# Four heads of ReLU attention weights on two engines: ScalarE takes a single bank and the pair, VectorE a bank of its own

## The chip, the cores and the metric

The kernel runs on one core of a Trainium2 chip. The metric is the device time of one execution in microseconds (us). A core has TensorE (PE, matrix products into PSUM), VectorE (DVE), ScalarE (ACT) and GpSimd (POOL), each with its own queue of instructions, and SyncE (SP), which issues DMAs. PSUM banks hold 128 x 512 numbers of four bytes here.

## The reference

Four layers follow each other on x of shape (4, 1024, 256): a gated attention in groups of 64, a low-rank feed-forward, a ReLU attention with 16 heads, and a mixture of eight experts. Each is wrapped as `x + layernorm(f(layernorm(x)))`. The change lies in the third:

```
scores = einsum('bhqd,bhkd->bhqk', q, k) / sqrt(16)
w = relu(scores)
attn = w / (sum(w, axis=-1) + 1e-6)
out = einsum('bhqk,bhkd->bhqd', attn, v)
y = layernorm(x + out @ w_out + b_out)
```

There are 4 rows (batch entries) of 1024 tokens, and 16 heads of width 16.

## The kernel before

**Stages.** The first two layers run to about 420 us of the span, the ReLU attention from there to about 1000 us, and the experts to the end. The attention is one long loop whose order is written out by hand for TensorE, VectorE and ScalarE: instructions stand in each engine's queue in the order in which the program calls them.

**Tiling.** For each of 4 rows there are 2 blocks of 512 queries, for each block 4 groups of 4 heads, and for each group 8 tiles of 128 keys: 256 steps in all. In the last block the queries are taken in two halves of 256, each with two key tiles in a step. `scores` (L1501) makes the scores of one step: 128 keys by 512 queries for each of four heads, in four PSUM banks. Two of them are single tiles of one bank (`singles`, tag `s`, a ring of three that the side work's small products share). The other two are one tile of two banks (`pair`, tag `d`, a ring of two). Then ReLU copies the scores into `w` in SBUF, a ring of three. `weigh` (L1527) multiplies `w` with the values into `po`, a single PSUM bank that collects the eight key tiles of a group. The values have a column of ones beside them, so `po` also holds the sums for the division.

**Order.** A step calls `scores` for itself and `finish` for the step two before. When the step that is finished is the last of its group, `finish` also transposes `po` into `turned` on VectorE (L1577). The first `weigh` of the next group overwrites `po` and must wait for that. Later parts of the same work divide by the sums (L1257 to L1259: `den`, `even`), transpose back (L1267: `oT`), project (L1288: `pt`), add and normalize (L1298 to L1320: `y`, `x`, with statistics at L1125 to L1132), and make the inputs of the experts' gate (L1349: `tpg`, L1352: `hTg`, L1364: `pg`). The next row's keys, queries and values (L392 to L441) are made in between. These parts wait in two lists: `beside` for pieces with TensorE work, `rest` for the others. A running account of how late each engine is (`late`, with costs written by hand) says when a part of `rest` may go.

**Heads by engine.** `heads_on_act` chooses how many of the four ReLUs ScalarE takes in a step:

```
if piece is not None and piece.tensor > 1.5:
    return 4
if late[1] > 0.0 or any(part.ready() and part.takes[1] for part in rest):
    return 2
return 3 if piece is None and at_end or last and len(rest) > 0 else 2
```

With a large side piece for TensorE it takes all four. It takes three where no piece is due and a group's last step is being finished, and in the last row while `rest` holds parts. Otherwise it takes two. The account's costs (`HEADS`) depend on that number. They are the same before and after.

With two heads, ScalarE takes the two singles (L1510) and VectorE the pair in one instruction (L1515). With four, ScalarE takes the singles and then the pair in one instruction (L1512). With three, ScalarE takes the singles and the first bank of the pair in three instructions (L1510), VectorE the second bank (L1515).

Of the kernel before, what the change touches and what calls it, by code (L numbers as in the profile page):

```python
# [13 lines left out]
AF = mybir.ActivationFunctionType  # L14
ALU = mybir.AluOpType
# [59 lines left out]
def kernel(  # L75
# [32 lines left out]
    nc = tc.nc  # L108
# [993 lines left out]
    with ExitStack() as st3:  # L1102
# [386 lines left out]
        def scores(row, qh, q2, halves, g, kt, on_act):  # L1489

            t, r = divmod(g, 2)
            n = TB // halves
            q0 = q2 * n
            w = wts.tile([P, 4, TB], F32, tag="w", name="w")
            singles = [ps.tile([P, TB], F32, tag="s", name="sc1", bufs=3) for _ in range(2)]
            pair = ps.tile([P, 2, TB], F32, tag="d", name="sc2", bufs=2)
            for m in range(halves):
                for part in (1, 0):
                    for j, sc in enumerate((*singles, pair[:, 0, :], pair[:, 1, :])):
                        rows = slice(32 * j, 32 * (j + 1))  # L1500
                        nc.tensor.matmul(  # L1501
                            sc[:, m * n : (m + 1) * n],
                            lhsT=row["kT"][t][rows, r, (kt + m) * P : (kt + m + 1) * P],
                            rhs=row["q"][qh, t][rows, r, part, q0 : q0 + n],
                            start=(part == 1),
                            stop=(part == 0),
                        )

            for j, sc in enumerate((*singles, pair[:, 0, :])[: 2 if on_act == 4 else on_act]):
                nc.scalar.activation(w[:, j, :], sc, AF.Relu)  # L1510
            if on_act == 4:
                nc.scalar.activation(w[:, 2:4, :], pair, AF.Relu)  # L1512
            else:
                j = on_act - 2
                nc.vector.tensor_scalar(w[:, 2 + j : 4, :], pair[:, j:2, :], 0.0, None, ALU.max)  # L1515
            return w

        def weighed(halves, r):
# [94 lines left out]
        def ends(at):  # L1613

            return at[6] == KT - at[4]

        def heads_on_act(piece, at_end, last):
# [6 lines that stand above are left out]
# [8 lines left out]
        for b in range(B):  # L1632
            after = open_row(None if b else next_hs, last=b + 2 == B) if b + 1 < B else None
            for qh in range(BPB):
# [13 lines left out]
                for q2 in range(halves):  # L1648
                    for g in range(NG):
                        for kt in range(0, KT, halves):  # L1650
                            Part.now += 1
                            piece = piece_for(waiting[0]) if len(waiting) > 1 else None
                            on_act = heads_on_act(piece, len(waiting) > 1 and ends(waiting[0]), row["last"])
                            w = scores(row, qh, q2, halves, g, kt, on_act)
                            waiting.append((row, b, qh, q2, halves, g, kt, w))
                            step = kt // halves
                            if step == 1 and g % 2 == 0:
                                if g == 0 and q2 == 0:
                                    fetch_queries(row, qh, 1)
                                elif g and halves == 1:  # L1660
                                    fetch_queries(*((row, 1) if qh == 0 else (after, 0)), 0)
                            for i, us in enumerate(HEADS[on_act]):
                                late[i] -= us
                            if len(waiting) > 2:
                                go_on_with_oldest(piece)
                            else:
                                go_on()
                            late[:] = [max(x, 0.0) for x in late]
# [574 lines left out]
```

## Time and profile before

| | before |
|---|---|
| median of 3 runs (lowest to highest) | 1534.33 us (1531.61 to 1535.67) |
| profiled execution: its time / its span | 1538.66 / 1536.9 us |
| mean granted TensorE clock | 0.984 |
| busy share of the span: PE, DVE, ACT, POOL | 95%, 57%, 46%, 32% |
| attention, 420 to 1000 us: PE, DVE, ACT busy | 551.1, 408.0, 400.9 of 580 us |
| steps with two, three, four heads on ScalarE | 152, 53, 51 |

A row of the profile names the source line, the engine, the operation, the tiles as out<-in, the shape and the count; then the busy time in us and the mean in ns, then how long the engine was idle just before these instructions, and what ended most of that. The page has the busy parts, the queues, the chain that ended last and the costliest groups. The trace also answers for a stretch: busy time, who waited for whom, and the instructions in order of time. A time of day such as 479.54 is counted in us from the start of the span. "PE po L1527 <- DVE turned L1577" reads: the matmuls into `po` at line 1527 waited for VectorE's write of `turned` at line 1577.

### The profile page before, as it was taken

The page shows a single profiled execution, that of the slowest core. Times are in us where ns is not written, and L with a number is a line of the kernel's source. Part 1 is how long each engine was busy: PE and PEld are TensorE (multiplying, and loading weights), DVE is VectorE, ACT ScalarE, POOL GpSimd, SP SyncE. Part 2 cuts the span into 40 slices and gives each one's busy share as a digit, 9 for nine tenths or more (in the row PEclk, how much of TensorE's full clock was granted, in tenths as well). Part 3 has the DMA queues.
Part 4 walks back from the last instruction along what each step waited for, and adds up shares of the span by engine and source line. Part 5 has one row for each costly group of instructions (what it writes and reads, how often), then busy time and mean ns, then how long its engine had stood idle before and what let it go on. Part 6 is the DMA issues. An engine that isn't in the chain of part 4 may idle for free. (4 is left out here: it accounts for less than half of the span.)

```text
span 1536.9 us, 24162 instructions
## 1 busy us (share of the span) xinstructions
PE 1465.8 (95%) x9286; PEld 787.5 (51%) x9286; DVE 875.4 (57%) x2140; ACT 701.4 (46%) x1201; POOL 495.9 (32%) x627
## 2 busy tenths in 40 slices
PE   8999999999899999999999999859999999999996
PEld 4666666666432323332333224427656765665674
DVE  5455664556456588648874776775545631222145
ACT  4244455443466666766676787622121112112142
POOL 4122233223341214311432223303425243242554
PEclk9999999999999999999999999969999999999999
DMA  8400000003323221532154210151314233233264
GB/s 217 128 1 1 1 1 0 1 0 126 121 71 124 90 91 61 173 114 87 49 165 138 70 56 29 40 158 36 99 22 122 49 70 90 56 79 78 63 161 127
DMA packets 91886, 121.59 MB, mean 79 GB/s; under 512 B 24925, under 2 KB 64250, under 8 KB 91642
## 3 DMA queue, kind: packets, MB, share of 16 engines
q1 hardware_dynamic: 70000, 73.09, 15.1%
q0 software_dynamic: 21712, 46.94, 13.0%
q8 instruction: 73, 1.20, 0.3%
q14 instruction: 43, 0.35, 0.1%
q10 hardware_dynamic: 58, 0.01, 0.0%
HBM read 66.90 MB, written 53.12 MB: 78 GB/s over the span
## 5 line engine op out<-in xcount | busy, mean ns | idle before, releaser
L1510 ACT ACTIVATE w<-sc 128x512 f32<-128x512 f32 x565 | 303.8, 596 | 135.1 <-issue 44.4
L1527 PE MATMUL po<-w,vaug 128*17 128x512 f32 (+1 forms) x2304 | 271.6, 553 | 24.3 <-DVE turned L1577 24.2
L1515 DVE TENSOR_SCALAR w<-sc 128x1024 f32<-128x1024 f32 (+1 forms) x205 | 221.2, 1083 | 77.1 <-ACT w L1510 43.7
L2125 ACT ACTIVATE hid<-ph,mb 128x512 f32<-128x512 f32 (+1 forms) x136 | 90.0, 662 | 340.0 <-PE ph L2118 249.6
L2118 PE MATMUL ph<-xT,w 128*128 128x512 f32 (+1 forms) x544 | 229.6, 574 | 0.3 <-DVE xT L2101 0.3
L2135 PE MATMUL py<-w,hid 128*128 128x256 f32 x1024 | 229.7, 380 | 0.0
L2135 PEld LDWEIGHTS py<-w,hid 128*128 128x128 f32 x1024 | 191.8, 190 | 31.6 <-issue 7.0
L1501 PE MATMUL sc<-q,kT 32*128 32x512 f32 (+1 forms) x2304 | 192.2, 414 | 2.7 <-ACT vaug L441 1.0
L1501 PEld LDWEIGHTS sc<-q,kT 32*128 32x128 f32 x2304 | 86.8, 184 | 176.4 <-ACT w L1510 112.6
L2156 POOL DMA_INDIRECT acc_d<-y,idx x56 | 88.8, 1585 | 225.5 <-DVE y L2155 111.1
L2118 PEld LDWEIGHTS ph<-xT,w 128*128 128x128 f32 x544 | 99.8, 190 | 107.1 <-issue 98.1
L1527 PEld LDWEIGHTS po<-w,vaug 128*17 128x17 f32 x2304 | 41.8, 95 | 118.8 <-issue 72.3
L2154 DVE TENSOR_TENSOR y<-py,mb 128x256 f32<-128x256 f32 x56 | 23.5, 420 | 125.9 <-PE py L2135 116.5
L1926 POOL DMA_INDIRECT got<-tok_d,idx x64 | 66.3, 1037 | 62.6 <-DVE counts L1760 24.4
L724 PE MATMUL pg<-nT,wh 128*128 128x512 f32 x128 | 61.1, 610 | 1.5 <-ACT nT L663 1.5
L2101 DVE COPY xT<-tp 128x512 f32<-128x512 f32 (+1 forms) x34 | 22.2, 659 | 70.7 <-PE tp L2096 64.6
L850 PE MATMUL py<-wo,oT 128*128 128x256 f32 x256 | 61.9, 385 | 0.0
L740 PE MATMUL pv<-wh,nT 128*128 128x512 f32 x128 | 59.7, 593 | 0.0
L850 PEld LDWEIGHTS py<-wo,oT 128*128 128x128 f32 x256 | 47.3, 190 | 17.1 <-issue 9.6
L1512 ACT ACTIVATE w<-sc 128x1024 f32<-128x1024 f32 x51 | 52.7, 1032 | 0.0
L915 ACT ACTIVATE hid<-ph,vec 128x512 f32<-128x512 f32 x64 | 39.8, 685 | 27.4 <-PE ph L906 27.2
L588 POOL TENSOR_TENSOR x<-x,y 128x1024 f32<-128x1024 f32 x13 | 30.6, 2353 | 57.4 <-ACT y L577 57.3
(307 smaller groups left out, 2043.5 us busy)
## 6 DMA issues: line engine op xcount, KB each, us to landing
q<-q_d POOLq DMA_DIRECT2D x16, 1024.0 KB, 6.4
w<-in_L_ffn_W_dram SPq DMA_DIRECT2D x16, 1024.0 KB
q_d<-parts SPq DMA_DIRECT2D x48, 256.0 KB
kT<-k_d POOLq DMA_DIRECT2D x16, 512.0 KB, 4.1
k_d<-parts SPq DMA_DIRECT2D x24, 256.0 KB
acc_d<-logits SPq DMA_DIRECT2D x8, 512.0 KB
tok_d<-hg SPq DMA_DIRECT2D x32, 128.0 KB
x<-in_L_attn_x_dram SPq DMA_DIRECT2D x7, 512.0 KB
```

Of the source, the lines that this page charges most:

```text
L724: nc.tensor.matmul(pg, lhsT=wh[:, c, HID + e * P : HID + (e + 1) * P], rhs=d["nT"][:, c, :], start=(c == 0), stop=(c == DC - 1),)
L740: nc.tensor.matmul(pv, lhsT=d["nT"][:, c, i * P : (i + 1) * P], rhs=wh[:, c, 0:HID], start=(c == 0), stop=(c == DC - 1),)
L850: nc.tensor.matmul(py, lhsT=d["oT"][:, e, :], rhs=wo[:, e, :], start=(e == 0), stop=(e == EC - 1))
L1501: nc.tensor.matmul(sc[:, m * n : (m + 1) * n], lhsT=row["kT"][t][rows, r, (kt + m) * P : (kt + m + 1) * P], rhs=row["q"][qh, t][rows, r, p ...
L1510: nc.scalar.activation(w[:, j, :], sc, AF.Relu)
L1515: nc.vector.tensor_scalar(w[:, 2 + j : 4, :], pair[:, j:2, :], 0.0, None, ALU.max)
L1527: nc.tensor.matmul(po[32 * j : 32 * j + HD + 1, weighed(halves, r)], lhsT=row["v"][:, kt + m, HQ * t + 4 * r + j, :], rhs=w[:, j, m * n : ...
L1926: return nc.gpsimd.indirect_dma_start(out=dst, out_offset=None, in_=rows[:, :], in_offset=self.at_chunk(c), bounds_check=NT - 1, oob_is_er ...
L2118: nc.tensor.matmul(ph, lhsT=w1[:, c, f * P : (f + 1) * P], rhs=xT[u][:, c, h * n : (h + 1) * n], start=(c == 0), stop=(c == DC - 1),)
L2125: nc.scalar.activation(hid[:, f, h * n : (h + 1) * n], ph, AF.Gelu, bias=mb1[:, e * FC + f : e * FC + f + 1])
L2135: nc.tensor.matmul(py, lhsT=hid[:, f, i * P : (i + 1) * P], rhs=w2[:, f, :], start=(f == 0), stop=(f == FC - 1),)
L2156: scatter = nc.gpsimd.indirect_dma_start(out=acc_d[:, :], out_offset=lists[e].at_chunk(k), in_=y, in_offset=None, bounds_check=NT - 1, oob ...
```

## The change

In a step with three heads on ScalarE, ScalarE takes the first single bank and then the whole pair in one instruction of 128 x 1024, and VectorE takes the second single bank. Before, ScalarE took both singles and the first bank of the pair in three instructions, and VectorE the pair's second bank. Steps with two and four heads keep their instructions. The choice of the number of heads, and with it the order of all other work, is as before.

```
-            for j, sc in enumerate((*singles, pair[:, 0, :])[: 2 if on_act == 4 else on_act]):
-                nc.scalar.activation(w[:, j, :], sc, AF.Relu)
-            if on_act == 4:
+            nc.scalar.activation(w[:, 0, :], singles[0], AF.Relu)
+            if on_act == 3:
+                nc.vector.tensor_scalar(w[:, 1, :], singles[1], 0.0, None, ALU.max)
+            else:
+                nc.scalar.activation(w[:, 1, :], singles[1], AF.Relu)
+            if on_act > 2:
                 nc.scalar.activation(w[:, 2:4, :], pair, AF.Relu)
             else:
-                j = on_act - 2
-                nc.vector.tensor_scalar(w[:, 2 + j : 4, :], pair[:, j:2, :], 0.0, None, ALU.max)
+                nc.vector.tensor_scalar(w[:, 2:4, :], pair, 0.0, None, ALU.max)
             return w
```

## The prediction

> **What bounds the kernel now.** I read the page's first part, then busy time by stretch, then who waited for whom, and last the timeline around one such wait. TensorE is busy nearly all the span:
>
> ```profile
> PE 1465.8 (95%) x9286; PEld 787.5 (51%) x9286; DVE 875.4 (57%) x2140; ACT 701.4 (46%) x1201; POOL 495.9 (32%) x627
> ```
>
> So only TensorE's idle time can be won unless its work changes, and the edit changes none of that. The edited lines run from 420 to 1000 us. Four stretches of that stage add up to:
>
> ```profile
> sum 580.00, PE 551.13 PEld 198.53 DVE 407.97 ACT 400.92 POOL 172.67; mean PE 137.78 PEld 49.63 DVE 101.99 ACT 100.23 POOL 43.17
> ```
>
> TensorE idles 580.0 - 551.1 = 28.9 us there: no gain can be much larger. Its waits, in the view of waits by engine over that stage, begin with one line that holds nearly all of it; below it are VectorE's, from the same view (us in total, times, longest):
>
> ```profile
> PE po L1527 <- DVE turned L1577: 24.2, 22, 1.5
> ...
> DVE w L1515 <- ACT w L1510: 43.7, 42, 2.0
> DVE w L1515 <- PE sc L1501: 31.8, 45, 3.0
> ```
>
> TensorE waits 22 times for `turned`, the transpose that empties `po` before the next group of heads may overwrite it. VectorE in its turn waits 42 times for ScalarE's ReLU. The groups by shape say which VectorE ReLU that is:
>
> ```profile
> L1510 ACT ACTIVATE w<-sc 128x512 f32<-128x512 f32 x565 | 303.8, 596 | 135.1 <-issue 44.4 <-ACT w L1510 41.7 <-PE sc L1501 37.3
> L1515 DVE TENSOR_SCALAR w<-sc 128x1024 f32<-128x1024 f32 x152 | 184.8, 1220 | 33.3 <-PE sc L1501 31.8 <-ACT hT L393 0.4
> L1512 ACT ACTIVATE w<-sc 128x1024 f32<-128x1024 f32 x51 | 52.7, 1032 | 0.0
> L1515 DVE TENSOR_SCALAR w<-sc 128x512 f32<-128x512 f32 x53 | 36.6, 690 | 43.8 <-ACT w L1510 43.7
> L1577 DVE STREAM_TRANSPOSE turned<-po 128x512 f32<-128x512 f32 x28 | 19.8, 708 | 5.5 <-PE po L1527 5.5
> ```
>
> The 53 one-bank ReLUs are the steps with three heads on ScalarE (152 have two, 51 four). They alone wait for ScalarE; the 152 two-bank ones wait for the matmuls. The timeline of one such step shows the chain:
>
> ```profile
> 477.12 0.74 PE L1501 MATMUL sc<-q,kT 32*128 32x512 f32 x8
> 477.78 1.05 PE L1527 MATMUL po<-w,vaug 128*17 128x512 f32 x8
> 477.93 1.58 ACT L1510 ACTIVATE w<-sc 128x512 f32<-128x512 f32 x3 [0.57 <-ACT w L1510]
> 478.76 0.74 PE L1501 MATMUL sc<-q,kT 32*128 32x512 f32 x8
> 479.54 0.69 DVE L1515 TENSOR_SCALAR w<-sc 128x512 f32<-128x512 f32 x1 [1.95 <-ACT w L1510]
> ...
> 480.15 0.71 DVE L1577 STREAM_TRANSPOSE turned<-po 128x512 f32<-128x512 f32 x1
> 480.91 1.05 PE L1527 MATMUL po<-w,vaug 128*17 128x512 f32 x8 [1.41 <-DVE turned L1577]
> ```
>
> The scores are complete at 477.86 and `po` at 478.83, but VectorE starts its ReLU at 479.54, when the third ScalarE ReLU has ended (479.51), and `turned` stands behind it. TensorE has finished the next scores at 479.50 and stands for 1.41 us.
>
> **What the Trainium skill says.** "PSUM — Partial Sum Buffer", section on bank collisions: two engines may not touch one bank and quadrant at a time, but on different banks they run clean together. The trace agrees: two-bank ReLUs run on VectorE beside ScalarE's at 1.22 and 0.60 us. Nothing in the banks thus demands the 1.6 us wait, which goes with the shared tile `pair`. The same page, "Engine vs sequencer instructions": the queues of ScalarE and VectorE are strict FIFO; so `turned` cannot pass the waiting ReLU, as seen above. "ScalarE: Activation LUTs", "What ACT_TABLE_LOAD costs": an ACTIVATE with immediates takes 186 ns + 0.833 ns per element, and neighbours overlap by about 93 ns. That gives 612 and 1039 ns; the trace has 596 and 1032.
>
> **The change part by part.** Only the 53 three-head steps change. The built order of instructions is otherwise the same on every engine: TensorE, POOL and SP keep all their instructions and DMAs, and nothing moves past anything.
>
> (1) *ScalarE*: 3 x 0.596 becomes 0.596 + 1.032; less overlaps of about 0.11 (three in 1.58 us above) 1.58 becomes 1.52, so 53 x 0.06 = 3 us of ScalarE time. Worth 0: it idles 0.57 us ahead of such a step.
>
> (2) *VectorE's ReLU* keeps its size (0.69 us), but reads a tile of its own. In the built program it waits for its matmul and for the older user of its `w` buffer, no longer for this step's ScalarE. It can start some 0.15 us after the matmuls (a two-bank one started at 476.36 after scores that ended at 476.20): 478.0 in place of 479.54. It ends at 478.7, before `po` is complete. Then `turned` starts 0.07 after `po` (elsewhere 461.79 to 461.86), takes 0.71, and TensorE follows 0.05 later: 478.83 + 0.83 = 479.66. TensorE is due at 479.50, so 0.16 of the 1.41 stays: **what is late next is `turned` itself**.
>
> *Stretch 420 to 860.* Of 13.6 us in 12 stalls, 0.54 and 0.22 stand behind another VectorE queue (two-bank ReLUs) and stay. Ten follow a three-head ReLU, 12.9 us: eight of 1.40 or 1.41, two of 0.81, where TensorE has other work between and nothing stays. Ahead of all ten VectorE had waited for ScalarE at least 1.19 us. Saved: 12.9 - 8 x 0.16 = 11.6.
>
> *Stretch 860 to 1000* (the last row, 43 of the 53 steps; 10 stalls, 10.6 us). One stall of 0.74 follows two-bank ReLUs. Nine follow a three-head one: 1.48, 0.82, 1.35, 1.35, 1.07, 1.07, 1.08, 1.12, 0.47, 9.8 together. Here VectorE also has layer-norm work, and its wait ahead of the nine ReLUs was only 0, 0.54, 0.12, 0.38, then 1.57, 0.97, 0.76, 1.56, 0.17. Capped by these and by the end of `po`, 5.1 go. But earlier ReLUs of the stretch waited too (27.8 us in 32 waits), and that time moves the queue up: with it all go but 0.16 in three places and a little elsewhere, 9.3. I take 8, nearer the upper end, because the queue before the four weakest shows ReLUs that waited 1.83, 1.13, 0.82 and 0.60.
>
> (3) *Other waits behind the same ReLU*: 0.74 as named; 0.53 (`sc` for `y`, at 974.17), 0.25 (`pt` for `oT`, at 933.68); and the hand-over at 995.05, where the ReLU waited 0.70 and the last layer-norm chain runs behind it. From 0 to 2.2; I take 1.5.
>
> (4) *New waits.* In the built order 28 score matmuls and 7 of the side work's (`tpg`, `pt`, `tp`) now wait for VectorE's ReLU where they waited for ScalarE's, as the single bank is released there; 29 lose a wait for VectorE on `pair`. Scores reuse it two steps (3.3 us) later: hidden behind two steps of TensorE work. The side work may come about 1 us later. No row shows its cost: at least 0 (a gain beyond (2) has no source), at most 7 x 0.5 = 3.5 if VectorE is half a us late every time. I take 1.
>
> Sum: 11.6 + 8 + 1.5 - 1 = **20 us**. Against the profiled execution, 1538.7 us (span 1536.9 and 1.8 around it), that is 1518.7; it ran 4.3 above the median, 1534.3, which goes to **1514.3**. After 1000 us the work depends on TensorE's arrival, so the gain is carried to the end.
>
> **The rivals.** (A) *VectorE's own queue takes the wait's place* in the last row: only the stretch before 860 gains, less 1 to 3 for new waits: 9 to 11, about 1524. For it: 11 of the 53 ReLUs did not wait. Against: the 27.8 us of waits there. (B) *No measurable change*: VectorE still waits for ScalarE, through `w`, which both still write. Then only part (1) is left and the time is 1534. Against: in two-head steps both write one `w` and VectorE waits only for TensorE. (C) *Slower*: the single bank, now released by VectorE, is late where ScalarE's was not. It decides once VectorE reaches its ReLU over 1 us late for side work, or 2.5 us late for scores: 35 waits at 1 us cost 35 against the 20, about 1549. For it: VectorE is 70% busy in this stage. Against: today's `pair` is released by VectorE later still, and no stall of TensorE names it.
>
> **How the numbers follow.** Forecast 0.76, A 0.12, B 0.06, C 0.06. The forecast's ends: 11.6 + 5.1 + 0 - 1 = 15.7, and 11.6 + 9.3 + 2.2 = 23.1: 1511 to 1519. With A's centre and 2 us by which runs scatter (1531.6 to 1535.7) it becomes 1509 to 1523. A measurement of this kernel tells about 0.3%, 4.6 us, from no change: faster 0.88 (forecast and A), same 0.06, slower 0.06.
>
> **What would show it.** Right: the one-bank VectorE ReLU waits for `sc` and not for ScalarE; "po <- turned" falls from 24.2 to some 5 us, mostly pieces of 0.1 to 0.2, and 0.54 and 0.22 remain; TensorE's busy time stays near 1466. Wrong: "DVE w <- ACT w" still near 40 us (B); stalls after 860 as long as now with VectorE busy before them (A); new stalls of `tpg`, `pt` or `sc` for VectorE's `w` (C).

## The result, and the profile after

The changed kernel takes 1510.5 us (median of 4 runs, 1508.3 to 1511.9); beside it the kernel before took 1535.0 (4 runs, 1531.6 to 1538.3). The ratio is 0.9839, with a 95% interval from 0.9814 to 0.9865: 24.5 us faster, with the interval 21 to 29. The forecast was 20 us and 1514.3, in a range from 1509 to 1523: the time lies inside the range, and the gain is larger than forecast. The profiled execution took 1511.9 us (span 1510.1, before 1536.9).

The new code is two lines longer, which shifts the line numbers: line 1527 of before is 1529 now, the transpose is at 1579, and the ReLUs are at 1509 and 1513 (ScalarE, one bank), 1515 (ScalarE, pair), 1511 (VectorE, one bank) and 1517 (VectorE, pair). First the busy time of the page:

```profile
PE 1461.7 (97%) x9286; PEld 786.1 (52%) x9286; DVE 876.1 (58%) x2140; ACT 698.2 (46%) x1148; POOL 496.5 (33%) x627
```

TensorE has the same 9286 matmuls and nearly the same busy time in 26.8 us less span. ScalarE has 53 instructions and 3.2 us less, as part (1) of the prediction had it. The waits of the attention stage, TensorE's first, then VectorE's (us in total, times, longest):

```profile
PE po L1529 <- DVE turned L1579: 2.6, 13, 0.5
...
DVE turned L1579 <- PE po L1529: 9.7, 20, 1.4
...
DVE w L1511 <- PE sc L1501: 5.9, 15, 1.0
```

TensorE waited 24.2 us for the transpose and now waits 2.6 (the forecast was some 5). "DVE w <- ACT w", 43.7 us before, is gone from the view; the one-bank ReLU waits for its matmul. And the transpose now waits for `po` in 20 places, 9.7 us (before 5.9 us in 7): the order of who is late has turned round. The groups by shape:

```profile
L1515 ACT ACTIVATE w<-sc 128x1024 f32<-128x1024 f32 x104 | 106.7, 1026 | 0.0
L1511 DVE TENSOR_SCALAR w<-sc 128x512 f32<-128x512 f32 x53 | 36.5, 688 | 6.7 <-PE sc L1501 5.9 <-ACT hTg L1352 0.4
L1579 DVE STREAM_TRANSPOSE turned<-po 128x512 f32<-128x512 f32 x28 | 20.0, 713 | 7.8 <-PE po L1529 7.7
```

VectorE's ReLU is no faster (688 ns against 690), it has only lost its wait: 6.7 us idle ahead of the 53, where there were 43.8. The step that the prediction showed, in the timeline after (start, duration, then the instruction):

```profile
475.60 0.74 PE L1501 MATMUL sc<-q,kT 32*128 32x512 f32 x8
...
476.27 1.05 PE L1529 MATMUL po<-w,vaug 128*17 128x512 f32 x8
476.42 0.60 ACT L1509 ACTIVATE w<-sc 128x512 f32<-128x512 f32 x1 [0.57 <-ACT w L1513]
476.46 0.69 DVE L1511 TENSOR_SCALAR w<-sc 128x512 f32<-128x512 f32 x1 [0.39 <-PE sc L1501]
476.91 1.02 ACT L1515 ACTIVATE w<-sc 128x1024 f32<-128x1024 f32 x1
...
477.39 0.72 DVE L1579 STREAM_TRANSPOSE turned<-po 128x512 f32<-128x512 f32 x1 [0.24 <-PE po L1529]
...
478.16 1.05 PE L1529 MATMUL po<-w,vaug 128*17 128x512 f32 x8 [0.17 <-DVE turned L1579]
```

Both engines start within 0.04 us of each other. The ReLU is done at 477.15, `po` at 477.32, and the transpose starts 0.07 later. Of the stall of 1.41 us 0.17 is left (0.16 was forecast).

**Where the time came from.** TensorE's matmuls are the same in number and order, so the two traces can be laid side by side, matmul by matmul; how far the second is ahead gives the gain up to any point.

| up to | ahead by, us | gained in between | what |
|---|---|---|---|
| 430 us of before | 1.5 | 1.5 | the granted clock, 0.85 from 424 to 444 us in the profile before, 0.93 in the one after |
| 849.4 (836.3 after) | 13.1 | 11.6 | ten stalls behind three-head ReLUs |
| 998.2 (971.5 after) | 26.7 | 13.6 | the last row: 9.7 in nine stalls, 3.9 elsewhere |
| the end | 26.8 | 0.1 | the experts: carried through |

The first 1.5 us are no work of the change: no three-head step lies there (the first is at 479.5 us of before).

### The profile page after: what moved, and what is told of

Its sections match the earlier page's. It is cut to its first block, busy times and chain, and to the rows that moved or that the text cites. A ratio compares the mean times of both kernels' runs of the same rounds, so it can differ in the third digit from the quotient of the medians.

```text
span 1510.1 us, 24181 instructions
## 1 busy us (share of the span) xinstructions
PE 1461.7 (97%) x9286; PEld 786.1 (52%) x9286; DVE 876.1 (58%) x2140; ACT 698.2 (46%) x1148; POOL 496.5 (33%) x627
## 5 line engine op out<-in xcount | busy, mean ns | idle before, releaser
L1517 DVE TENSOR_SCALAR w<-sc 128x1024 f32<-128x1024 f32 x152 | 185.1, 1222 | 36.2 <-PE sc L1501 33.8
L1509 ACT ACTIVATE w<-sc 128x512 f32<-128x512 f32 x256 | 152.9, 597 | 113.7 <-ACT w L1513 49.5
L1513 ACT ACTIVATE w<-sc 128x512 f32<-128x512 f32 x203 | 120.2, 592 | 0.0
L1515 ACT ACTIVATE w<-sc 128x1024 f32<-128x1024 f32 x104 | 106.7, 1026 | 0.0
L1928 POOL DMA_INDIRECT got<-tok_d,idx x64 | 66.6, 1041 | 62.9 <-DVE counts L1762 24.5
```

What stands on the lines that cost most here:

```text
L1509: nc.scalar.activation(w[:, 0, :], singles[0], AF.Relu)
L1513: nc.scalar.activation(w[:, 1, :], singles[1], AF.Relu)
L1517: nc.vector.tensor_scalar(w[:, 2:4, :], pair, 0.0, None, ALU.max)
L1928: return nc.gpsimd.indirect_dma_start(out=dst, out_offset=None, in_=rows[:, :], in_offset=self.at_chunk(c), bounds_check=NT - 1, oob_is_er ...
```

## The experiments

Each is timed against the kernel before. The first four ran together, as did the next four and the last two. Only the code of the three-head step or its place is shown; the line numbers differ by a few from kernel to kernel.

### 1. The old sharing, VectorE called first

```
+            if on_act == 3:
+                nc.vector.tensor_scalar(w[:, 3, :], pair[:, 1, :], 0.0, None, ALU.max)
             for j, sc in enumerate((*singles, pair[:, 0, :])[: 2 if on_act == 4 else on_act]):
                 nc.scalar.activation(w[:, j, :], sc, AF.Relu)
             if on_act == 4:
                 nc.scalar.activation(w[:, 2:4, :], pair, AF.Relu)
-            else:
-                j = on_act - 2
-                nc.vector.tensor_scalar(w[:, 2 + j : 4, :], pair[:, j:2, :], 0.0, None, ALU.max)
+            elif on_act == 2:
+                nc.vector.tensor_scalar(w[:, 2:4, :], pair, 0.0, None, ALU.max)
```

> The heads are shared out as before (ScalarE both singles and the pair's first bank in three instructions, VectorE the pair's second bank), but in a three-head step VectorE's ReLU is called ahead of ScalarE's. Theory (what cost the time was VectorE's wait for ScalarE, with the transpose of po behind it in VectorE's queue): the wait goes though the pair is still shared, TensorE's wait for the transpose falls from 24 us to 2 to 4 us, and the time is 1510 to 1514. Rival (a shared pair holds one engine up in either order): now ScalarE's third ReLU waits for VectorE's wherever VectorE is late, in about a fifth of the 53 steps by half a us or more, scores behind it come later, and the time is 1516 to 1522.

1509.0 us, ratio 0.9828 (0.9808 to 0.9849). VectorE's one-bank ReLU in the groups by shape, and one of ScalarE's waits:

```profile
L1510 DVE TENSOR_SCALAR w<-sc 128x512 f32<-128x512 f32 x53 | 36.4, 688 | 7.7 <-PE sc L1501 6.5 <-ACT hTg L1352 0.4 <-ACT w L1512 0.3
...
ACT w L1512 <- DVE w L1510: 2.4, 6, 0.7
```

The pair is still shared, VectorE reads one bank of it while ScalarE works on other banks, and the whole gain is there; TensorE waits 2.6 us for the transpose, as in the changed kernel. So a bank of its own is one way, not the reason: what counts is that VectorE does not come after ScalarE. It was the order of the two calls on one tile that had made VectorE the later. The tile still ties the two engines, now the other way round: in all 53 steps ScalarE's third ReLU begins only after VectorE's has ended (0.03 us later at the least). So the rival of this run does appear, but small: ScalarE stands for VectorE 2.4 us in six waits, where half a us in a fifth of the steps was its claim, and scores come visibly late behind it in one place only (near 933 us, 0.45 us). VectorE's ReLU mostly ends before ScalarE has finished its first two.

### 2. The new sharing, the pair in two ScalarE instructions

```
-            if on_act > 2:
+            if on_act == 3:
+                for j in range(2):
+                    nc.scalar.activation(w[:, 2 + j, :], pair[:, j, :], AF.Relu)
+            elif on_act == 4:
                 nc.scalar.activation(w[:, 2:4, :], pair, AF.Relu)
```

> The changed kernel, with the pair in a three-head step taken by ScalarE in two instructions of one bank rather than one of two. Theory (ScalarE's shorter work is worth nothing, the whole gain is the wait): ScalarE is 3 us busier, the time is within 1.5 us of the changed kernel's 1510.5. Rival (part of the gain is ScalarE's shorter step, above all in the last row where three-head steps follow each other at 1.58 us against TensorE's 1.65): 2 to 3 us slower, 1513.

1509.3 us, ratio 0.9829 (0.9812 to 0.9846), against 0.9839 for the change. The shorter ScalarE step is worth nothing that can be measured; with experiment 1 this leaves VectorE's wait as the cause of the gain, as far as the times can tell.

### 3. The change in the first three rows only

The first branch holds the new sharing, the second the old.

```
+            if not row["last"]:
...
+            else:
...
```

> The change in the first three rows only (10 steps); the last row keeps the old sharing (43 steps). Theory: ten stalls of 12.9 us shrink to eight of 0.17; with 0.1 us more for each stall where the pipeline had run dry, the time falls by 12 to 13 us, to 1522 to 1523. Rival (more than half of the gain comes from the last row's lighter VectorE queue): a fall of 8 us or less, 1527 or more.

1524.2 us, ratio 0.9922 (0.9906 to 0.9939): 10.4 us less in the medians, 9.4 to 14.4 by the interval. In its trace the eight stalls are 0.17 each and those of the last row stay as they were (1.49, 0.82, 1.35, 1.35, 1.07 and so on). TensorE's wait and one of VectorE's:

```profile
PE po L1538 <- DVE turned L1588: 12.7, 20, 1.5
...
DVE w L1526 <- ACT w L1521: 27.8, 32, 1.9
```

27.8 us in 32 waits is what the last row had in the kernel before. Laid side by side, the traces of the kernels before and after gave 11.6 for these ten steps; the time is 1.2 us above the expected 1523. The extra 0.1 us a stall that I had expected was not there in the eight stalls that shrank to 0.17 (1.41 to 0.17 brought 1.24); the two that went altogether gave 0.07 each (0.81 brought 0.88). The rival's "8 or less" lies outside the interval. So nearly half of the gain comes from ten steps, the rest from the last row's 43.

### 4. The change only where the transpose follows

The branches as in experiment 3; `group_end` is true where the step that is finished is the last of its group.

```
+            if group_end:
...
+            else:
...
```

> The change only in the 19 three-head steps with the transpose behind VectorE's ReLU; the other 34 of the last row keep the old sharing. Theory (VectorE's freed time carries over in the last row from one step to the next): four stalls of the last row stay for the most part (about 0.9, 0.3, 1.2 and 1.0 us, as VectorE comes to them late), and so do those behind other work; 4 to 6 us slower than the changed kernel, 1515 to 1517. Rival (only the ReLU ahead of each transpose matters): within 1.5 us of the changed kernel, 1511.

1514.0 us, ratio 0.9867 (0.9846 to 0.9888), 4.7 to 5.0 behind experiments 1 and 2, which ran with it: the theory holds, and the time lies just under the expected 1515 to 1517. One of the last row's stalls, in the timeline:

```profile
847.09 0.48 DVE L1320 SCALAR_TENSOR_TENSOR x<-y,rsc,x 128x256 f32<-128x256 f32 x1
847.48 0.69 DVE L1512 TENSOR_SCALAR w<-sc 128x512 f32<-128x512 f32 x1
848.09 0.71 DVE L1588 STREAM_TRANSPOSE turned<-po 128x512 f32<-128x512 f32 x1
...
848.85 0.62 PE L1538 MATMUL po<-w,vaug 128*17 128x512 f32 x4 [1.49 <-DVE turned L1588]
```

Here the ReLU has the new sharing and waits for nobody, but VectorE comes to it late, and TensorE still stands 1.49 us. In the changed kernel the same stall is 0.17. The earlier ReLUs' waits had made VectorE late: freed time does carry over from step to step.

### 5. Two heads on ScalarE in place of three

```
-                            w = scores(row, qh, q2, halves, g, kt, on_act)
+                            w = scores(row, qh, q2, halves, g, kt, 2 if on_act == 3 else on_act)
```

> The kernel before, with ScalarE taking two heads in the 53 steps where it took three (VectorE the whole pair in one instruction of 1.22 us, which waits for no ScalarE); the account of lateness and all else stay. Theory (in a wait-free step only VectorE's load and the end of po count): in the first three rows the ReLU ends 0.53 us later than in the changed kernel, the transpose about 0.25 later, and eight stalls of 0.17 become 0.41: 10 us saved there. In the last row VectorE gets 43 x 0.53 = 23 us more, on a queue that was already late in four stalls of nine, so little or nothing is saved there: 1521 to 1530. Rival (three heads on ScalarE are not needed at all once nothing waits for ScalarE): within 3 us of the changed kernel, 1510 to 1513.

1522.3 us, ratio 0.9916 (0.9897 to 0.9935). The first three rows gain nearly as expected (six of the eight stalls are 0.41 to 0.56, two 0.65 and 0.67; matmul by matmul 8.8 us where 10 were expected). In the last row VectorE is full; the stretch from 860 to 990 us (its length, then busy us of PE, PEld, DVE, ACT, POOL, each with its count; last the granted clock, the share of DMA and GB/s):

```profile
860.00:990.00 130.00, 121.49 (x1572) 55.07 (x1565) 114.70 (x226) 77.69 (x142) 44.06 (x83) 0.99 0.14 45
```

VectorE is busy 114.7 of 130 us, and stalls of 1.81, 1.25 and 1.03 us stand there. The third head on ScalarE is needed, but only without the wait: even two heads beat the old three.

### 6. The old sharing, the transpose ahead of the ReLU

In three-head steps at a group's end VectorE's ReLU, wait and all, is called behind the transpose:

```
-                nc.vector.tensor_scalar(w[:, 2 + j : 4, :], pair[:, j:2, :], 0.0, None, ALU.max)
+                held.append(
+                    lambda: nc.vector.tensor_scalar(w[:, 2 + j : 4, :], pair[:, j:2, :], 0.0, None, ALU.max)
+                )
+                if not (on_act == 3 and group_end):
+                    held.pop()()
...
                     po[:, weighed(halves, r)],
                 )
+                while held:
+                    held.pop()()
```

> The kernel before with its sharing of heads, but in three-head steps at a group's end VectorE's ReLU is called behind the transpose of po, not ahead of it; it still waits for ScalarE. Theory (the wait cost time only because the transpose stood behind it in the queue): TensorE's waits for the transpose fall as in the changed kernel in the first three rows (0.17 each) and to about 0.1 to 0.9 in the last row, where VectorE is late; VectorE still waits 20 to 40 us for ScalarE; 1512 to 1517. Rival (the ReLU's own lateness holds the later weighing): 1525 or more.

1514.4 us, ratio 0.9872 (0.9852 to 0.9892). TensorE hardly waits, and part of VectorE's wait for ScalarE is left. Below the waits, the step that the prediction showed:

```profile
PE po L1533 <- DVE turned L1583: 4.6, 14, 0.9
...
DVE w L1518 <- ACT w L1512: 16.9, 26, 1.9
...
475.07 0.74 PE L1503 MATMUL sc<-q,kT 32*128 32x512 f32 x8
475.20 0.72 DVE L1583 STREAM_TRANSPOSE turned<-po 128x512 f32<-128x512 f32 x1 [1.31 <-PE po L1533]
475.84 0.69 DVE L1518 TENSOR_SCALAR w<-sc 128x512 f32<-128x512 f32 x1
...
475.97 0.62 PE L1533 MATMUL po<-w,vaug 128*17 128x512 f32 x4 [0.17 <-DVE turned L1583]
```

20 of the 24 us come back. VectorE's ReLU begins no earlier than it did, 0.77 us after TensorE's next scores (478.76 and 479.54 in the kernel before, 0.78), but the transpose now lies in the time that VectorE had stood waiting, and TensorE's 1.41 us become 0.17. At the 19 group ends VectorE thus stands idle for ScalarE only 0.4 us in all, 22.0 before. The 16.9 us that are left (20 to 40 were expected) stand nearly all at steps with no transpose behind the ReLU; they still make VectorE late in the last row, where stalls of 0.89, 0.54 and 0.31 us stay. The wait cost time by what stood behind it in VectorE's queue.

### 7. The change, with every ReLU behind the transpose

At each group's end, in two-head steps too, the ReLU is called behind the transpose, by the same `held` list in the changed kernel.

> The changed kernel, and VectorE's ReLU called behind the transpose of po at every group's end, in two-head steps too. Theory (0.17 us of each stall is the transpose itself after po's end): the stalls of 0.54 and 0.22 behind two-head ReLUs go, those of 0.17 stay; 1 us at most, so no difference that can be measured, 1508 to 1511. Rival (a later ReLU makes scores wait for its bank): 1513 or more, with waits of sc for VectorE's w.

1515.2 us, ratio 0.9868 (0.9848 to 0.9888): a miss, 4.7 us above the changed kernel's own median. The two did not run together and the intervals of their ratios overlap, so the reading rests on the traces. The stalls of 0.54 and 0.22 went as expected, but new ones came (timeline):

```profile
575.84 0.72 DVE L1583 STREAM_TRANSPOSE turned<-po 128x512 f32<-128x512 f32 x1 [0.57 <-PE po L1533]
...
576.48 0.65 DVE L1513 TENSOR_SCALAR w<-sc 128x512 f32<-128x512 f32 x1
...
577.28 0.63 PE L1349 MATMUL tpg<-ident,hg 128*128 128x128 f32 x4 [0.84 <-DVE w L1513]
```

The gate's transposes take the single bank that this ReLU empties, and the ReLU now comes late. This is the prediction's rival C at work, in the side work and not in the scores: 0.84 us for `tpg`, 0.84 for `tp`, and only one wait of 0.15 for scores. In the changed kernel, with the ReLU first, no idle time of TensorE's matmuls is put down to L1511. Of 3.9 us between the two profiled executions 1.6 were there before the first wait for the transpose, 1.3 of them from 424 to 431 us, where the granted clock dips, and are no work of the edit.

### 8. The change only where no transpose follows

The condition of experiment 4 turned round.

> The change only in the 34 three-head steps without a transpose behind VectorE's ReLU; the 19 at a group's end keep the old sharing. Theory (the loss sits in the ReLU ahead of the transpose): all stalls of 1.0 to 1.5 us stay at 1.1 to 1.5, only the waits of pt and sc for VectorE and some of the end go; 1530 to 1534. Rival (a lighter VectorE queue is itself worth half of the last row's 13 us): 1528 or less.

1532.3 us (14 runs), ratio 0.9987 (0.9975 to 0.9998).

```profile
PE po L1538 <- DVE turned L1588: 24.3, 21, 1.4
...
DVE w L1526 <- ACT w L1521: 31.3, 19, 2.5
```

The freed 34 steps alone bring about 2 us (0.3 to 3.8 by the interval). The stalls behind three-head ReLUs stay, at 1.1 to 1.4 each (0.8 in three). The 19 ReLUs that are still held waited 31.3 us for ScalarE, 1.65 each, where they had waited 22.0 in the kernel before: what is freed ahead of a held ReLU is spent waiting there. With the 19 freed as well, the same 34 are worth 3.5 to 5 us (experiment 4 against the change and against experiments 1 and 2).

### 9 and 10. Two-head steps reordered, beside the changed kernel again

In the changed kernel, only the nine two-head steps at a group's end have the ReLU behind the transpose.

> The changed kernel, with VectorE's ReLU called behind the transpose only in the nine two-head steps at a group's end (three-head steps keep it ahead). Theory (the stalls of 0.54 and 0.22 come from the two-bank ReLU ahead of the transpose, and the side work's new waits only from a one-bank ReLU called late): both stalls go, no wait of tpg or tp for VectorE's w appears, 0.8 to 1 us less in the trace, too little for the times to show: within 1.5 us of the changed kernel run beside it. Rival (any later ReLU holds the scores): 2 us or more slower.

> The changed kernel itself, on the same chip as the nine-step variant. Theory: 1508 to 1512, TensorE's waits for the transpose 2.6 us in all, as in its first profile; what differs between executions is the stretch just after 424 us, where the granted clock dips, by 1 to 4 us. Rival (the first profile was a lucky one): 1514 or more.

1512.9 us, ratio 0.9846 (0.9829 to 0.9863), beside the changed kernel's 1512.1, 0.9836 (0.9819 to 0.9853). No difference can be measured. The stalls of 0.54 and 0.22 went, but one of 0.17 became 0.36, a new one of 0.15 (`sc` for VectorE's `w`) came, and `tpg` waited 1.2 us for POOL near the end where it had waited 0.6; the trace ends 1.1 us later, not 0.8 to 1 earlier. The changed kernel's repeat shows the 2.6 us of its first profile; its time is 24.7 below that of the kernel before on that chip (1536.8). None of these versions is measurably better than the changed kernel.

## Why the prediction was right, point by point

**The mechanism** stood as told: ScalarE's third ReLU, VectorE's ReLU, the transpose, TensorE. Experiments 1 and 6 break that chain at two different places without the change and get all of the gain (25.6 us) and most of it (19.8). The sizes were less good: three terms missed, all on the same side.

**Part (1)**, ScalarE worth 0: shown by experiment 2.

**Part (2), 420 to 860 us:** 11.6 forecast, 11.6 in the aligned traces. The remainder of 0.16 measured 0.17, and it is the transpose, as said: it now waits for `po`.

**Part (2), the last row:** 8 forecast, 9.7 measured. This term was too small. The carry-over was complete: all nine stalls fell to 0.17 or to nothing, where I had left a discount. Experiment 4 shows that it is carry-over, as without it stalls of 1.49, 1.15 and 0.69 stay. The three remainders of 0.16 that were forecast are there, 0.17 each. Stalls that went altogether were worth some 0.07 more than their recorded idle time (1.07 to 1.12 recorded, 1.14 to 1.19 gained).

**Part (3)**, other waits behind the same ReLU: 1.5 forecast, at most 2.2, measured 3.9. The three named ones gave 0.6, 0.6 and 0.5 and the end of the row 1.3, where 0.7 had been recorded; 0.5 came near 905 us and 0.4 in smaller pieces. Near 905 us the matmuls show no idle time, but the weight loads do. In the kernel before:

```profile
PEld sc L1501 <- DVE w L1515: 0.3, 1, 0.3
```

This wait ended at 905.44: the loads for the two heads of `pair` stood until VectorE's two-bank ReLU, itself late in its queue, had freed the tile. Two heads' matmuls had begun at 904.94, so TensorE counted as busy; in the changed kernel all four heads begin together. The prediction said that no stall of TensorE names the release of `pair`: that holds for matmuls and not for this weight load.

**Part (4)**, new waits: 1 forecast, no idle time of the matmuls found. The waits themselves came, in the weight loads of the scores:

```profile
PEld sc L1501 <- DVE w L1511: 9.3, 14, 0.9
```

They passed while earlier matmuls still ran. Experiment 7 makes such waits of the side work cost 0.84 each, more than the 0.5 of the forecast's bound, by calling the ReLU behind the transpose.

The sum is 11.6 + 9.7 + 3.9 = 25.2 against 20; 1.5 of the profiles' 26.7 is the clock. The medians differ by 24.5. That is more than the 23.1 to which the prediction's own terms reach at most: the time lies within the stated range only by the 2 us that were added for scatter. At its other end the range stops at 1523, a little short of rival A's centre of 1524, which it was meant to take in. The rivals fell with the traces: A, as in the last row the stalls went; B, as VectorE no longer waits for ScalarE, though both still write one `w`; C, as no idle time of the matmuls names the new ReLU.

## What to carry to other kernels

When two engines each take a part of one step's work, look at what stands behind the later one in its queue: a wait that this engine could well afford can hold the transpose or copy that frees the bank of the engine that bounds the kernel. Separate tiles, the other order of the two calls, or the urgent instruction put ahead removed 25, 26 and 20 us here. Where steps follow each other closely, count the waits of the steps before too: they decide how late the queue comes to the one that matters.

## What the runs showed of the hardware

The granted TensorE clock around the start of the attention differs between executions of the same instructions: from 424 to 444 us it was 0.84 (experiment 3), 0.85 (the kernel before), 0.93 (the changed kernel) and 1.00 (experiments 4 and 6). TensorE's first wait for the transpose then lies at 475.9 us in experiment 4 and at 480.0 in experiment 3, though up to there the two kernels are the same. Of these 4 us 2.8 arise between 424 and 431 us, and 1.2 between 400 and 404, where the clocks differ too (from 400 to 424 us 0.99 in experiment 4, 0.93 in experiment 3). That is as much as several of these experiments were to tell apart, and is why the gain was read from traces laid side by side, matmul by matmul.
